# First two graphs of a two-layer graph network: logits as feature columns, broadcasts over all 128 rows, bias from a broadcast tile, products of zeros between stages

## The chip, the core and the metric

The kernel runs on one core of a Trainium2 chip. The metric is device time in microseconds, of one launch over all 64 graphs. A profile is one more execution, taken by the hardware profiler. PE is TensorE (PEld its weight loads), DVE is VectorE, ACT is ScalarE, POOL is GpSimd and SP is the engine whose queue issues nearly all DMAs. Everything is float32, and a matmul of float32 appears in the trace as two records.

## What is computed

There are 64 independent graphs of N = 256 nodes with F = 512 features. Layer 0 is graph attention with H = 8 heads of U = 64 units, layer 1 is dense self-attention with added graph terms; each ends in a residual and a layer norm. Cut to what matters here:

```
feats   = einsum('bnf,hfu->bhnu', X, W)            # layer 0
e_self  = einsum('bhnu,hu->bhn', feats, a_self)
e_neigh = einsum('bhnu,hu->bhn', feats, a_neigh)
dense   = leaky_relu(e_self[..., :, None] + e_neigh[..., None, :], 0.2)
att     = softmax(dense + NEG_BIG * (1 - A), axis=-1)
out     = relu(einsum('bhij,bhju->bhiu', att, feats) + b)
x       = layernorm(x + out)
# layer 1: q, k, v = x @ W_qkv; softmax(q k^T) * LA + LG * adj + LD * exp(-adj), times v;
# x = layernorm(x + result @ W_out + b_out)
```

## The kernel before, in words

**Steady state.** Graphs are handled one after another, in a software pipeline written out by hand: `attention0_beside_projections1(b)` and `attention1_beside_projections0(b)` for b from 2 on mix layer 0 of graph b with layer 1 of graphs b-1 and b-2. There the products of the projections are the seven of Strassen's scheme (`seven`, tiles `pq_p`, `pv_p`, `pf_p`, `po_p`), each `halved` into two matmuls of 64 columns that lie beside each other in the array (line 87).

**The start.** Graphs 0 and 1 go through layer 0 in `start()` and `second_beside_first()` with plain products, because weight sums and the first logits are not there yet. `do(stage, b, step)` records one step, and `in_order()` after it fixes the order of the source on every engine[...]. So the order written in `start()` is the order of PE, DVE, ACT and POOL, and of SP's DMA queue.

The steps of the start that matter below, for graph b = 0 and 1:

- `attention_vectors(g)` (lines 411 to 431) spreads the vectors a_self and a_neigh of four heads over 128 partitions: a matmul of one row of ones, `sel[0:1, H]`, with one row `arow` (line 423, tile `pa_bc`). Ahead of it stand four products of a tile of zeros, `idle` (line 420).
- `logit_weights(g, c, step)` (lines 433 to 449) multiplies the layer's weights by those vectors (`prod`, line 440, on DVE or POOL) and sums over the units (line 446, DVE) into `WA["columns"]`. `vectors_placed` (line 451) copies the sums by ACT into two spare columns per head of the weight tiles `wf`.
- `features(t, g)` (from line 664) makes the features of node tile t and head group g: a matmul of one row that puts the bias in, then four chunks c of 128 input features. `xT_rows` (line 532) turns x first.
- `logits()` (from line 571, matmuls at 575 and 585) makes e_self and e_neigh in matmuls of their own: x against `columns` as rows (40 output rows of 256) and as columns (8 wide).
- `maxima` (lines 594 to 609) takes the row maximum of e_neigh, an exponential, and a small matmul that spreads the maximum (line 599). `factors(g)` (lines 611 to 625) spreads one row per head over 128 partitions: a matmul of 8 rows per head (line 622, tile `pg`). `columns` makes two small exponentials.
- `scaled(h)` (line 688, ACT) moves features from PSUM to SBUF times a factor; `weights(h)` (line 725, DVE, tile `pT`) makes the attention weights of a head; `product(g, t)` (line 748, PE, tile `av`) applies them; `rec0`, `norm0`, `end`, `squares`, `norm` finish layer 0.
- `proj1` with `from_rows` (line 871), `qk` (tile `pq_p`) and `combine_weights1` (lines 278 to 284, DVE sums of weights that `load_weights1` brings in) starts layer 1 of graph 0 beside the second head group of graph 1.

```
def halved(dst, lhsT, rhs, **flags):
    for r in range(2):
        cols = slice(r * (P // 2), (r + 1) * (P // 2))
        matmul(dst[cols], lhsT[:, cols], rhs, **flags)
```

## Time and profile before

| | us |
|---|---|
| median of three runs (2837.8 to 2844.21) | 2844.15 |
| profiled execution, whole | 2843.23 |
| its span, first to last instruction | 2841.4 |
| PE busy in the span | 2823.1 (99%) |
| DVE busy | 2559.0 (90%) |
| ACT busy | 1807.5 (64%) |
| POOL busy | 254.3 (9%) |

From 160 us to 2760 us PE is busy all but 0.7 us; the first layer-1 product (`pq_p`) starts at 64.08 us, and the last 80 us hold one graph's tail. In the table of windows each row gives a stretch, and for each engine the busy time with the number of records, then the granted TensorE clock (1.00 is full speed) and the DMA's share and rate. In the timeline a row has its start, the time to its end, engine, line, operation, tile written and tiles read, and the number of merged records. The chain of work that ended last gives start, share of the time, engine, tile and line of each piece.

### The profile page before, as it was taken

What the parts mean: (1) busy time and instruction counts of PE and PEld (TensorE: products, weight loads), DVE (VectorE), ACT (ScalarE), POOL (GpSimd) and SP (SyncE); (2) the same over time, 40 slices, a digit from 0 to 9 for tenths busy, and PEclk for the clock granted to TensorE, in tenths of its full rate; (3) what the DMA queues carried; (4) which work ended last, traced back from release to release, by engine and by line L of the source; (5) the groups of instructions that cost most, each with busy time, mean ns of one, the idle gap of its engine ahead of it and who ended that gap; (6) DMA issues with size and microseconds to landing.
All of it is one profiled execution on the core that took longest, in us unless ns stands there. A gap on an engine that the chain in (4) does not pass through costs nothing.

```text
span 2841.4 us, 93467 instructions
## 1 busy us (share of the span) xinstructions
PE 2823.1 (99%) x39110; PEld 2241.4 (79%) x39110; DVE 2559.0 (90%) x5125; ACT 1807.5 (64%) x5054; POOL 254.3 (9%) x531
## 2 busy tenths in 40 slices
PE   9999999999999999999999999999999999999998
PEld 6787787887887878887878877888888778778875
DVE  4899999999999999999999999999999999999984
ACT  3656666666666666666666666666666666666664
POOL 1001000000100100010010001001001000100101
PEclk8999999999999999999999999999999999999999
DMA  5445445455454454454454544544544544544532
GB/s 115 102 128 133 126 138 122 132 144 121 130 146 120 127 137 123 131 139 122 136 129 129 140 121 132 144 121 126 140 128 128 139 120 134 136 125 136 125 112 70
DMA packets 773473, 362.82 MB, mean 128 GB/s; under 512 B 689359, under 2 KB 691391, under 8 KB 757054
## 3 DMA queue, kind: packets, MB, share of 16 engines
q1 hardware_dynamic: 770942, 356.33, 47.9%
q8 instruction: 310, 5.08, 0.8%
q14 instruction: 109, 0.89, 0.1%
q10 hardware_dynamic: 2112, 0.52, 0.1%
HBM read 288.37 MB, written 68.13 MB: 125 GB/s over the span
## 4 chain that ended last, share of the span: by engine, by line
PE 98%; DVE 1%; ACT 1%; issue 0%; POOL 0%; POOLq 0%; DVEq 0%; ACTq 0%
PE pq_p L87 27%; PE po_p L87 14%; PE pf_p L87 14%; PE pv_p L87 13%; PE av L748 8%; PE pz L909 8%; PE av L1038 7%; PE pd L948 2%; PE pf L87 1%; PE pr L539 1%; PE po L87 0%; PE pg L622 0%; DVE p L1019 0%; PE pa_bc L423 0%; PE pl L585 0%
## 5 line engine op out<-in xcount | busy, mean ns | idle before, releaser
L87 PE MATMUL pq_p<-hC,wqk_sb 128*64 128x128 f32 x8192 | 470.2, 273 | 1.7 <-ACT qk L337 1.7
L87 PEld LDWEIGHTS pq_p<-hC,wqk_sb 128*64 128x64 f32 x8192 | 448.9, 137 | 3.1 <-ACT qk L337 2.5
L725 DVE SCALAR_TENSOR_TENSOR pT<-gb,ccol,at 128x256 f32<-128x256 f32 x992 | 403.0, 477 | 17.2 <-ACT ccol L639 17.2
L87 PE MATMUL pq_p<-hT,wqk_sb 128*64 128x128 f32 x6144 | 357.9, 273 | 0.7 <-DVE qk L340 0.5
L87 PEld LDWEIGHTS pq_p<-hT,wqk_sb 128*64 128x64 f32 x6144 | 342.3, 137 | 10.5 <-DVE qk L340 0.7
L928 ACT ACTIVATE p<-pz,hide 128x512 f32<-128x512 f32 x638 | 333.2, 629 | 8.9 <-PE pz L909 1.7
L1019 DVE TENSOR_TENSOR p<-p,rb 128x1024 f32<-128x1024 f32 x252 | 298.9, 1206 | 3.4 <-DMA rb<-rs 3.4
L1028 DVE TENSOR_TENSOR p<-p,ct 128x1024 f32<-128x1024 f32 x252 | 299.0, 1207 | 0.2
L769 ACT ACTIVATE x<-av,rec 128x64 f32<-128x64 f32 x1024 | 223.7, 335 | 64.8 <-DVE rec L761 64.8
L748 PE MATMUL av<-v,pT 128*64 128x65 f32 x8192 | 253.6, 222 | 0.6
L87 PE MATMUL pf_p<-wf_sb,xC 128*64 128x264 f32 x1984 | 254.0, 386 | 0.0
L748 PEld LDWEIGHTS av<-v,pT 128*64 128x64 f32 x8192 | 249.8, 138 | 2.6 <-issue 2.0
L87 PE MATMUL pv_p<-wv_sb,hC 128*64 128x256 f32 x2048 | 244.4, 379 | 2.6 <-ACT v L337 2.5
L337 ACT COPY qk<-pq_p 128x512 f32<-128x512 f32 x256 | 148.8, 581 | 152.2 <-PE pq_p L87 148.5
L1038 PE MATMUL av<-p,v 128*64 128x256 f32 x2016 | 241.2, 380 | 2.1 <-DVE p L1028 2.1
L688 ACT ACTIVATE v<-v 128x64 f32<-128x64 f32 x992 | 243.0, 336 | 0.0
L909 PE MATMUL pz<-qk 64*128 64x256 f32 x2048 | 239.4, 384 | 0.0
L337 ACT COPY v<-pv_p 128x256 f32<-128x256 f32 x256 | 95.7, 374 | 221.0 <-PE pv_p L87 221.0
L87 PE MATMUL po_p<-wo_sb,oC 128*64 128x256 f32 x1984 | 235.2, 379 | 0.0
L391 POOL TENSOR_SCALAR rstd_l<-rstd_l 128x2 f32<-128x2 f32 (+1 forms) x130 | 95.6, 736 | 1536.1 <-ACT junk L380 1535.9
L909 PEld LDWEIGHTS pz<-qk 64*128 64x128 f32 x2048 | 192.9, 187 | 45.6 <-issue 25.0
L940 DVE SCALAR_TENSOR_TENSOR both<-p 128x512 f32<-128x512 f32 x256 | 172.2, 674 | 45.1 <-ACT p L928 44.8
(169 smaller groups left out, 4480.7 us busy)
## 6 DMA issues: line engine op xcount, KB each, us to landing
rb<-rs SPq DMA_DIRECT2D x63, 1024.0 KB
gb<-gs SPq DMA_DIRECT2D x62, 1028.0 KB
hs<-x SPq DMA_DIRECT2D x64, 512.0 KB
xb<-in_x_dram SPq DMA_DIRECT2D x252, 128.0 KB
x<-in_x_dram SPq DMA_DIRECT2D x63, 512.0 KB
y<-hs SPq DMA_DIRECT2D x63, 512.0 KB
out_dram<-y SPq DMA_DIRECT2D x63, 512.0 KB
hb<-hs SPq DMA_DIRECT2D x248, 128.0 KB
```

Of the source, the lines that this page charges most:

```text
L87: matmul(dst[cols], lhsT[:, cols], rhs, **flags)
L337: nc.scalar.copy(out[COPIES[p]], dst)
L688: nc.scalar.activation(v[:, :U], src, AF.Copy, scale=v[:, U : U + 1])
L725: nc.vector.scalar_tensor_tensor(pT[h][:, j, :], GB[b][h], CCOL[b][:, j, h : h + 1], AT[b][:, j, :], op0=ALU.max, op1=ALU.mult,)
L748: matmul(av[r * half : (r + 1) * half, k, :], pT[h][:, j, i : i + half], V0[b][:, j, h, :UA], start=(j == 0), stop=(j == T - 1),)
L769: nc.scalar.activation(X1[b][:, t, h * U : (h + 1) * U], av[:, k, :U], AF.Copy, scale=REC0[g][:, t, k : k + 1],)
L909: matmul(pz[r][:, j, :], QK[b][rows, g, 1, j * P : (j + 1) * P], QK[b][rows, g, 0, :], start=True, stop=True,)
L928: nc.scalar.activation(to, of, AF.Exp, bias=hide[:, j, b : b + 1], scale=U**-0.5,)
L940: nc.vector.scalar_tensor_tensor(both[g], p[:, :, 0, :], TINY, p[:, :, 1, :], op0=ALU.add, op1=ALU.add)
L1019: nc.vector.tensor_mul(p, p, REC[b][:, k : k + 2, g // 2, :] .unsqueeze(2) .to_broadcast([P, 2, T, N]),)
L1028: nc.vector.tensor_add(p, p, CT[b].unsqueeze(1).to_broadcast([P, 2, T, N]))
L1038: matmul(av[0][r * U : (r + 1) * U, g % 2, :], V1[b][:, j, 2 * g + r, :], PROBS[b][g][:, r, j, :], start=(j == 0), stop=(j == T - 1),)
```

## The change

It touches `start()`, the steps that `start()` records for graphs 0 and 1, and one step of the second stage. Nothing of the steady state is changed but where one set of weight sums is made.

- `sel`, `arow` and `grow` get 128 rows, with zeros where there were none, and the matmuls of `pa_bc`, `pg` and the small maximum's `sel` copy read all of them (the maximum's matmul itself keeps 8 rows). The memsets for it are on DVE and POOL; the rows of `arow` are loaded after x.
- The sums of `logit_weights` go directly into the spare columns of `wf`, and `features` takes all 66 columns per head: features and logits come out of one product of 264 columns. `logits()` loses its matmuls and becomes four small copies; four transposes (tile `pr`) turn the logits into rows.
- The bias matmul of one row inside `features` goes. `bias_rows` spreads the bias once (one matmul of 512 columns), and `copied` adds it while moving features out of PSUM (DVE); `scaled` then works on SBUF.
- `keep_busy(dst, n)` issues n products of the zero tile: 8 at the start in place of 4, 8 and 2 in graph 0's `maxima`, 6 in graph 1's.
- The order in `start()` is rewritten. Among others the second half of graph 1's factors, weights and scalings now stand behind the first `pq_p` products.
- `right_factors(wo_sb, ...)` (four DVE sums) moves from `second_beside_first()` into the stage of b = 2, and the tile `wo12` takes another buffer.

```diff
-    arow = wo_sb[0:1, 4:].rearrange("p k c f -> p k (c f)")
+    arow = wo_sb[:, 4:].rearrange("p k c f -> p k (c f)")
+    nc.vector.memset(arow[:, 0], 0.0)
+    nc.gpsimd.memset(arow[:, 1], 0.0)
+    nc.gpsimd.memset(arow[:, 2], 0.0)
...
-    sel = work.tile([H, H + 1, P], FT, tag="rb", name="sel", bufs=1)
+    sel = work.tile([P, H + 1, P], FT, tag="rb", name="sel", bufs=1)
...
-        wo12 = work.tile([P, C2, F2], FT, tag="pT", name="wo12", bufs=4)
+        wo12 = work.tile([P, C2, F2], FT, tag="p", name="wo12", bufs=5)
...
+    def bias_rows():
+        pb = WA["bias"].rearrange("p k h u -> p (k h) u")
+        matmul(
+            pb.rearrange("p h u -> p (h u)"), sel[:, H, :], arow[:, 2], start=True, stop=True
+        )
+        nc.scalar.copy(b0_bc[:, :, :U], pb)
+        in_order()
+
+    def keep_busy(dst, n):
+        for _ in range(n):
+            matmul(dst, idle, idle, start=True, stop=True)
...
             nc.vector.tensor_reduce(
-                WA["columns"][:, c, :, g * HG : (g + 1) * HG], WA.pop((g, c)), AX.X, ALU.add
-            )
+                wf[c // C2][g][:, c % C2, :, U:].rearrange("p h s -> p s h"),
+                WA.pop((g, c)),
+                AX.X,
+                ALU.add,
+            )
...
+        def logits(g):
...
+                nc.vector.tensor_copy(
+                    ROW["near"][:, t, :, g * HG : (g + 1) * HG],
+                    PF[t, g][:, :, U:].rearrange("p h s -> p s h"),
+                )
+        def maxima(part=None):
+            if part == 1:
+                matmul(ROW["max"], sel[:H, H, :], ROW["diag"], start=True, stop=True)
+                if b == 0:
+                    keep_busy(WA[1][:, 0, :2], 2)
+                return
...
+                    transpose(ps[:, s, t * P : (t + 1) * P], ROW["near"][:, t, s, :])
+            if b == 0:
+                keep_busy(WA[1][:, 0, :2], 8)
...
+                matmul(
+                    pg[:, k, :], sel[:, h + k, :], ROW["rows"][:, :N], start=True, stop=True
+                )
...
-                PF[t, g] = ps_tile([P, HG, U], f"pf_{b}_{t}_{g}")
-                halved(
-                    PF[t, g],
-                    sel[0:1, H, :],
-                    arow[:, 2, g * HG * U : (g + 1) * HG * U],
-                    start=True,
-                    stop=False,
-                )
+                PF[t, g] = ps_tile([P, HG, UX], f"pf_{b}_{t}_{g}")
...
+        def copied(t, g):
+            nc.vector.tensor_add(
+                halves(t, g)[:, :, :U],
+                PF.pop((t, g))[:, :, :U],
+                b0_bc[:, g * HG : (g + 1) * HG, :U],
+            )
```

The new order in `start()`, cut to its second half (`do` left out): `factors` of two heads, `scaled`, `weights` for graph 0's heads 0 to 3; `factors` for heads 4 to 7; `product` 0; `copied` for the second group; `xT` of graph 1; `rec0`, `scaled`, `masks`, `norm0`, `far`; `features` of graph 1's first group; `weights` 4 to 7; `product` 1; `logits` 0; `combine_weights1(0)`; `rec0`, `norm0` and `features` of the second group; `end`, `squares`, `copied`, `logits` 1, `norm`, `maxima`, six products of zeros, `norm`, `from_rows` 0, `copied`, the maximum, `columns`, `factors` 0 to 3, `shared`, `aT`, `pq_p` p1, `from_rows` 1, `far`, p2, `hC`, `combine_weights1(4)`, p6, `combine_weights1(1)`, `scaled` and `weights` 0 to 3, p5, p7, `combine_weights1(2)`, `factors` 4 to 7, `scaled` and `weights` 4 to 7, `shared`, p4, p3.

More of the change, by code (lines that the diff above doesn't have):

```diff
@@ L147, in load_rows @@
         nc.sync.dma_start(X[b], x[b].rearrange("(t p) f -> p t f", p=P))
+    rowmask = consts.tile([P, NB // B, N // B, B], FT, name="rowmask")
+    idle = rowmask[:, 0, : P // B].rearrange("p i b -> p (i b)")
+    nc.vector.memset(idle, 0.0)
     wo_sb = consts.tile([P, 7, C2, F2], FT, name="wo_sb")
-    arow = wo_sb[0:1, 4:].rearrange("p k c f -> p k (c f)")
-    for k, a in enumerate((a_self, a_neigh, b0)):
-        nc.sync.dma_start(arow[:, k, :], a.rearrange("h u -> (h u)").unsqueeze(0))
+    arow = wo_sb[:, 4:].rearrange("p k c f -> p k (c f)")
+    nc.vector.memset(arow[:, 0], 0.0)
+    nc.gpsimd.memset(arow[:, 1], 0.0)
+    nc.gpsimd.memset(arow[:, 2], 0.0)
     X[0] = io.tile([P, T, F], FT, tag="hb", name="x_0", bufs=1)
@@ L156 @@
         nc.sync.dma_start(X[0][:, t, :], x[0, t * P : (t + 1) * P, :])
+    for k, a in enumerate((a_self, a_neigh, b0)):
+        nc.sync.dma_start(arow[0:1, k, :], a.rearrange("h u -> (h u)").unsqueeze(0))
     wf_sb = consts.tile([P, 7, C2, HG, UX], FT, name="wf_sb")
@@ L171 @@
     load_wf(nc.sync, 1)
-    sel = work.tile([H, H + 1, P], FT, tag="rb", name="sel", bufs=1)
+    sel = work.tile([P, H + 1, P], FT, tag="rb", name="sel", bufs=1)
     nc.vector.memset(sel[:, H, :], 1.0)
-    rowmask = consts.tile([P, NB // B, N // B, B], FT, name="rowmask")
-    idle = rowmask[:, 0, : P // B].rearrange("p i b -> p (i b)")
-    nc.vector.memset(idle, 0.0)
     load_adj(0)
@@ L180 @@
     nc.vector.memset(b0_bc, 0.0)
-    nc.sync.dma_start(
-        b0_bc[:, :, :U], b0.rearrange("h u -> (h u)").partition_broadcast(P)
-    )
     wqk_sb = consts.tile([P, 7, C2, F], FT, name="wqk_sb")
@@ L191 @@
     nc.vector.tensor_copy(
-        sel[:, :H, :], ident[:H, :H].unsqueeze(2).to_broadcast([H, H, P])
+        sel[:, :H, :], ident[:, :H].unsqueeze(2).to_broadcast([P, H, P])
     )
@@ L212, in masks @@
             maskf = work.tile([NB, N], FT, tag="far", name="maskf", bufs=1)
+            MASK["rows"] = maskf
             nc.scalar.copy(maskf, mask_sb)
+        elif step == 1:
+            maskf = MASK.pop("rows")
             nc.vector.transpose(maskz, maskf)
@@ L414, in attention_vectors @@
         if g == 0:
-            WA["psum"] = psum.tile([P, 2, 2, HG, U], FT, tag="sc", name="pa_bc", bufs=2)
             WA["sbuf"] = io.tile([P, 2, 2, HG, U], FT, tag="x1", name="a_bc", bufs=1)
-            WA["columns"] = work.tile([P, C, 2, B], FT, tag="hC", name="wa", bufs=1)
-            nc.vector.memset(WA["columns"], 0.0)
-            for _ in range(4):
-                matmul(WA["psum"][:, 0, 0, :2], idle, idle, start=True, stop=True)
+        pa = WA[g] = psum.tile([P, 2, 2, HG, U], FT, tag="sc", name=f"pa_bc_{g}", bufs=2)
+        WA["bias"] = pa[:, 1]
+        pa = WA[g] = pa[:, 0]
+        if g == 0:
+            keep_busy(pa[:, 0, :2], 8)
         for k in range(2):
@@ L423, in attention_vectors @@
             matmul(
-                WA["psum"][:, g, k].rearrange("p h u -> p (h u)"),
-                sel[0:1, H, :],
+                pa[:, k].rearrange("p h u -> p (h u)"),
+                sel[:, H, :],
                 arow[:, k, cols],
@@ L429, in attention_vectors @@
             )
-        nc.scalar.copy(WA["sbuf"][:, g], WA["psum"][:, g])
+        nc.scalar.copy(WA["sbuf"][:, g], pa)
         in_order()
+    def bias_rows():
[8 more added lines that the diff above has]
+            matmul(dst, idle, idle, start=True, stop=True)
     def logit_weights(g, c, step):
@@ L438, in logit_weights @@
             )
-            engine, src = (nc.gpsimd, "sbuf") if c % 2 or g and c else (nc.vector, "psum")
+            engine, src = (
+                (nc.gpsimd, WA["sbuf"][:, g]) if c % 2 else (nc.vector, WA[g])
+            )
             engine.tensor_mul(
@@ L442, in logit_weights @@
                 wf[c // C2][g][:, c % C2, :, :U].unsqueeze(1).to_broadcast([P, 2, HG, U]),
-                WA[src][:, g],
+                src,
             )
@@ L446, in logit_weights @@
             nc.vector.tensor_reduce(
-                WA["columns"][:, c, :, g * HG : (g + 1) * HG], WA.pop((g, c)), AX.X, ALU.add
-            )
-        in_order()
-    def vectors_placed():
-        for k in range(2):
-            for g in range(2):
-                nc.scalar.copy(
-                    wf[k][g][:, :, :, U:].rearrange("p c h s -> p c s h"),
-                    WA["columns"][:, k * C2 : (k + 1) * C2, :, g * HG : (g + 1) * HG],
-                )
+                wf[c // C2][g][:, c % C2, :, U:].rearrange("p h s -> p s h"),
+                WA.pop((g, c)),
+                AX.X,
+                ALU.add,
+            )
         in_order()
@@ L569, in proj0 @@
         ROW = {}
-        def logits():
-            pl = ps_tile([P, 2, N], f"pl_{b}")
-            for c in range(C):
-                matmul(
-                    pl[: B + H, 0],
-                    WA["columns"][:, c].rearrange("p s k -> p (s k)")[:, : B + H],
-                    xT[:, c],
-                    start=(c == 0),
-                    stop=(c == C - 1),
-                )
-            near = pl[:, 1, : T * H].rearrange("p (t h) -> p t h", h=H)
-            for t in range(T):
-                for c in range(C):
-                    matmul(
-                        near[:, t],
-                        xT[:, c, t * P : (t + 1) * P],
-                        WA["columns"][:, c, 1, :H],
-                        start=(c == 0),
-                        stop=(c == C - 1),
-                    )
-            ROW.update(logits=pl, near=near, max=pl[:, 1, T * H : (T + 1) * H])
+        def logits(g):
+            if g == 0:
+                ROW["near"] = small.tile([P, T, 2, H], FT, tag="lg", name=f"lg_{b}", bufs=1)
+            for t in range(T):
+                nc.vector.tensor_copy(
+                    ROW["near"][:, t, :, g * HG : (g + 1) * HG],
+                    PF[t, g][:, :, U:].rearrange("p h s -> p s h"),
+                )
@@ L594, in maxima, with cleared @@
+        def cleared():
+            ROW["rows"] = small.tile([P, N + 1], FT, tag="grow", name=f"grow_{b}", bufs=1)
+            nc.gpsimd.memset(ROW["rows"], 0.0)
         def maxima(part=None):
             if part == 1:
-                nd = ROW["nd"] = small.tile([P, T, H], FT, tag="nd", name=f"nd_{b}", bufs=2)
-                nc.vector.tensor_copy(nd, ROW["near"])
-                matmul(ROW["max"], sel[:, H, :], ROW["diag"], start=True, stop=True)
+                matmul(ROW["max"], sel[:H, H, :], ROW["diag"], start=True, stop=True)
+                if b == 0:
+                    keep_busy(WA[1][:, 0, :2], 2)
@@ L600, in maxima @@
                 return
-            pl = ROW["logits"]
-            grow = small.tile([H, N + 1], FT, tag="grow", name=f"grow_{b}", bufs=1)
+            pr = psum.tile([P, 2, 2, N], FT, tag="sc", name=f"pr_{b}", bufs=2)
+            ps = pr[:H, 0]
+            for s in range(2):
+                for t in range(T):
+                    transpose(ps[:, s, t * P : (t + 1) * P], ROW["near"][:, t, s, :])
+            if b == 0:
+                keep_busy(WA[1][:, 0, :2], 8)
+            grow = ROW["rows"]
@@ L603, in maxima @@
             nb = small.tile([H, 1], FT, tag="nb", name=f"nb_{b}", bufs=2)
-            nc.vector.tensor_reduce(grow[:, N : N + 1], pl[B : B + H, 0], AX.X, ALU.max)
-            nc.vector.tensor_scalar_mul(nb, grow[:, N : N + 1], -0.8)
-            nc.scalar.activation(grow[:, :N], pl[:H, 0], AF.Exp, bias=nb, scale=-0.8)
+            nc.vector.tensor_reduce(grow[:H, N : N + 1], ps[:, 1, :], AX.X, ALU.max)
+            nc.vector.tensor_scalar_mul(nb, grow[:H, N : N + 1], -0.8)
+            nc.scalar.activation(grow[:H, :N], ps[:, 0, :], AF.Exp, bias=nb, scale=-0.8)
@@ L607, in maxima @@
             diag = small.tile([H, H], FT, tag="diag", name=f"diag_{b}", bufs=1)
-            nc.vector.tensor_scalar_mul(diag, ident[:H, :H], grow[:, N : N + 1])
-            ROW.update(rows=grow, diag=diag)
-        def factors(part=None):
-            grow = ROW["rows"]
-            if part != 1:
-                nc.vector.tensor_scalar(
-                    grow[:, :N], grow[:, :N], 1.0, TINY, op0=ALU.min, op1=ALU.max
-                )
-                GB[b] = []
-            for g in range(2) if part is None else (part,):
-                pg = psum.tile([P, HG, N], FT, tag="sc", name=f"pg_{b}_{g}", bufs=2)
-                for k in range(HG):
-                    matmul(
-                        pg[:, k, :], sel[:, g * HG + k, :], grow[:, :N], start=True, stop=True
-                    )
-                    GB[b].append(pg[:, k, :])
+            nc.vector.tensor_scalar_mul(diag, ident[:H, :H], grow[:H, N : N + 1])
@@ new lines, in maxima, with clamped, busy, factors @@
+            ROW.update(diag=diag, max=pr[:, 1, 0, :H])
+        def clamped():
+            nc.vector.tensor_scalar(
+                ROW["rows"][:H, :N], ROW["rows"][:H, :N], 1.0, TINY, op0=ALU.min, op1=ALU.max
+            )
+            GB[b] = []
+        def busy(n):
+            ROW["pg"] = psum.tile([P, HG, N], FT, tag="sc", name=f"pg_{b}_0", bufs=2)
+            keep_busy(ROW["pg"][:, 0, :P], n)
+        def factors(h, n):
+            if "pg" in ROW:
+                pg = ROW.pop("pg")
+            elif n == 2:
+                pg = ps_tile([P, n, N], f"pg_{b}_{h}")
+            else:
+                pg = psum.tile([P, n, N], FT, tag="sc", name=f"pg_{b}_{h}", bufs=2)
+            for k in range(n):
+                matmul(
+                    pg[:, k, :], sel[:, h + k, :], ROW["rows"][:, :N], start=True, stop=True
+                )
+                GB[b].append(pg[:, k, :])
@@ L627, in columns @@
         def columns():
-            if b > 1:
-                nd = small.tile([P, T, H], FT, tag="nd", name=f"nd_{b}", bufs=2)
-            else:
-                nd = ROW["nd"]
+            nd = small.tile([P, T, H], FT, tag="nd", name=f"nd_{b}", bufs=2)
             nc.vector.tensor_sub(
                 nd,
-                V0[b][:, :, :, U + 1] if b > 1 else nd,
+                V0[b][:, :, :, U + 1] if b > 1 else ROW["near"][:, :, 1, :],
                 (gb[:, :, N] if b > 1 else ROW["max"])
@@ L666, in features @@
             if c is None or c == 0:
-                PF[t, g] = ps_tile([P, HG, U], f"pf_{b}_{t}_{g}")
-                halved(
-                    PF[t, g],
-                    sel[0:1, H, :],
-                    arow[:, 2, g * HG * U : (g + 1) * HG * U],
-                    start=True,
-                    stop=False,
-                )
+                PF[t, g] = ps_tile([P, HG, UX], f"pf_{b}_{t}_{g}")
             for c in range(C) if c is None else (c,):
@@ L678, in features @@
                     xT[:, c, t * P : (t + 1) * P],
-                    wf[c // C2][g][:, c % C2, :, :U],
-                    start=False,
+                    wf[c // C2][g][:, c % C2],
+                    start=(c == 0),
                     stop=(c == C - 1),
                 )
+        def copied(t, g):
[4 more added lines that the diff above has]
+            )
         def scaled(h):
@@ L686, in scaled @@
                 v = V0[b][:, t, h]
-                src = v[:, :U] if b > 1 else PF[t, h // HG][:, h % HG]
-                nc.scalar.activation(v[:, :U], src, AF.Copy, scale=v[:, U : U + 1])
+                nc.scalar.activation(v[:, :U], v[:, :U], AF.Copy, scale=v[:, U : U + 1])
         return dict(
+            copied=copied,
+            cleared=cleared,
             logits=logits,
             maxima=maxima,
+            busy=busy,
+            clamped=clamped,
             factors=factors,
@@ L1212, in start @@
         attention_vectors(1)
+        do("proj0", 0, "xT_rows")
         for step in (
@@ L1222, in start @@
             (1, 1, 0),
+            (1, 0, 0),
+            (1, 3, 0),
+            (1, 0, 1),
             (1, 2, 0),
-            (1, 0, 0),
-            (1, 0, 1),
             (1, 1, 1),
-            (1, 3, 0),
             (1, 2, 1),
-            (1, 3, 1),
         ):
             logit_weights(*step)
-        do("proj0", 0, "xT_rows")
-        for c in range(C):
-            for t in range(T):
-                do("proj0", 0, "features", t, 0, c)
-        masks(0)
-        masks(1)
-        do("proj0", 0, "logits")
-        for c in range(2):
-            do("proj0", 0, "features", 0, 1, c)
-        do("proj0", 0, "maxima")
+            if step[2] == 1:
+                for t in range(T):
+                    do("proj0", 0, "features", t, *step[:2])
+            if step == (1, 2, 0):
+                bias_rows()
+                masks(0)
+            if step == (1, 2, 1):
+                do("proj0", 0, "logits", 0)
+        logit_weights(1, 3, 1)
+        for t in range(T):
+            do("proj0", 0, "features", t, 1, 3)
         do("proj0", 0, "aT")
@@ L1245, in start @@
         combine_weights1 = load_weights1()
+        do("proj0", 0, "logits", 1)
+        do("proj0", 0, "cleared")
+        do("proj0", 0, "maxima")
+        do("proj0", 0, "copied", 0, 0)
+        do("proj0", 0, "copied", 1, 0)
         do("proj0", 0, "maxima", 1)
-        for c in range(2, C):
-            do("proj0", 0, "features", 0, 1, c)
+        do("proj0", 0, "clamped")
         do("proj0", 0, "columns")
-        do("proj0", 0, "factors", 0)
-        do("proj0", 0, "factors", 1)
-        do("proj0", 0, "features", 1, 1)
         for h in range(HG):
+            if h % 2 == 0:
+                do("proj0", 0, "factors", h, 2)
             do("proj0", 0, "scaled", h)
             do("attend0", 0, "weights", h)
-        do("proj0", 0, "far", 1)
+        do("proj0", 0, "factors", HG, HG)
         for t in range(T):
             do("attend0", 0, "product", 0, t)
+        do("proj0", 0, "copied", 0, 1)
+        do("proj0", 0, "copied", 1, 1)
         do("turned", 1, "xT")
@@ L1263, in start @@
             do("proj0", 0, "scaled", h)
+        masks(1)
+        masks(2)
         do("attend0", 0, "norm0", 0, 0)
         do("attend0", 0, "norm0", 0, 1)
-        do("attend0", 0, "weights", HG)
-        do("attend0", 0, "weights", HG + 1)
-        do("proj0", 1, "logits")
-        vectors_placed()
-        do("proj0", 1, "maxima")
-        do("attend0", 0, "weights", HG + 2)
-        do("attend0", 0, "weights", HG + 3)
+        do("proj0", 0, "far", 1)
         for t in range(T):
             do("proj0", 1, "features", t, 0)
-        do("proj0", 1, "maxima", 1)
+        for h in range(HG, H):
+            do("attend0", 0, "weights", h)
         for t in range(T):
             do("attend0", 0, "product", 1, t)
-        do("proj0", 1, "columns")
-        do("proj0", 0, "shared", 0)
-        do("proj0", 1, "aT")
-        do("proj0", 1, "far", 0)
-        do("proj0", 1, "factors", 0)
+        do("proj0", 1, "cleared")
+        do("proj0", 1, "logits", 0)
+        combine_weights1(0)
         do("attend0", 0, "rec0", 1)
@@ L1285, in start @@
             do("attend0", 0, "norm0", 1, t)
+            do("proj0", 1, "features", t, 1)
+        for t in range(T):
             do("attend0", 0, "end", tiles[t])
-        do("attend0", 0, "squares", tiles[0])
-        do("attend0", 0, "squares", tiles[1])
         for t in range(T):
-            do("proj0", 1, "features", t, 1)
-        do("proj0", 1, "factors", 1)
-        for h in range(HG):
-            do("proj0", 1, "scaled", h)
+            do("attend0", 0, "squares", tiles[t])
+        do("proj0", 1, "copied", 0, 0)
+        do("proj0", 1, "copied", 1, 0)
+        do("proj0", 1, "logits", 1)
         do("attend0", 0, "norm", tiles[0])
+        do("proj0", 1, "maxima")
+        do("proj0", 1, "busy", 6)
         do("attend0", 0, "norm", tiles[1])
         do("proj1", 0, "from_rows", 0)
+        do("proj0", 1, "copied", 0, 1)
+        do("proj0", 1, "copied", 1, 1)
+        do("proj0", 1, "maxima", 1)
+        do("proj0", 1, "clamped")
+        do("proj0", 1, "columns")
+        do("proj0", 1, "factors", 0, HG)
+        do("proj0", 0, "shared", 0)
+        do("proj0", 1, "aT")
+        do("proj1", 0, "qk", "p1")
         do("proj1", 0, "from_rows", 1)
@@ L1299, in start @@
         load_rows(1)
-        for h in range(HG):
-            do("attend0", 1, "weights", h)
-        do("proj1", 0, "qk", "p1")
-        combine_weights1(0)
-        combine_weights1(4)
+        do("proj0", 1, "far", 0)
         do("proj1", 0, "qk", "p2")
         do("proj1", 0, "hC")
+        combine_weights1(4)
         do("proj1", 0, "qk_add", 11)
@@ L1309, in start @@
         combine_weights1(1)
+        for h in range(HG):
+            do("proj0", 1, "scaled", h)
+            do("attend0", 1, "weights", h)
+        do("proj1", 0, "qk", "p5")
+        do("proj1", 0, "qk", "p7")
+        combine_weights1(2)
+        do("proj0", 1, "factors", HG, HG)
+        do("proj1", 0, "qk_add", 22)
+        for h in range(HG, H):
+            do("proj0", 1, "scaled", h)
+        for h in range(HG, H):
+            do("attend0", 1, "weights", h)
         do("proj0", 0, "shared", 1)
@@ L1312, in start @@
         load_adj(2)
-        do("proj1", 0, "qk", "p5")
-        do("proj1", 0, "qk", "p7")
-        for h in range(HG, H):
-            do("proj0", 1, "scaled", h)
-            do("attend0", 1, "weights", h)
-        combine_weights1(2)
-        do("proj1", 0, "qk_add", 22)
         do("proj1", 0, "qk", "p4")
@@ L1338, in second_beside_first @@
         do("turned", 2, "xC")
-        for t in range(T):
-            do("attend0", b, "norm0", 0, t)
+        do("attend0", b, "norm0", 0, 0)
         do("proj1", 0, "values", "p1")
+        do("attend0", b, "norm0", 0, 1)
         for t in range(T):
@@ L1372, in second_beside_first @@
         do("proj0", 2, "add", 11)
-        right_factors(wo_sb, WO["12"], (0, 1))
         do("proj0", 2, "add", 12)
@@ L1378, in second_beside_first @@
         do("proj0", 2, "rows")
-        right_factors(wo_sb, WO.pop("12"), (2, 3))
         do("proj0", 2, "broadcast", 0)
@@ L1449, in attention0_beside_projections1 @@
         do("attend1", b - 3, "residual")
+        if b == 2:
+            right_factors(wo_sb, WO["12"], (0, 1))
         do("proj1", b - 1, "values", "p6")
@@ L1455, in attention0_beside_projections1 @@
             do("attend1", b - 3, "sum_up", t)
+        if b == 2:
+            right_factors(wo_sb, WO.pop("12"), (2, 3))
         if b + 2 < NB:
```

## The prediction

> **What bounds the kernel now.** I read the page first, for the engines over the span:

> ```profile
> PE   9999999999999999999999999999999999999998
> PEclk8999999999999999999999999999999999999999
> ```

> PE is full from the first slice to the last, and nothing else is; but one slice has a clock below nine tenths, the first 71 us. So time is PE time, and the change lies where PE is full and slow. The chain of waits agrees: PE holds 98% of it. The windows of 10 us show where (columns: busy of PE, PEld, DVE, ACT, POOL with records, granted clock, DMA share, GB/s):

> ```profile
> 20.00:30.00 10.00, 9.95 (x50) 6.62 (x49) 1.84 (x7) 4.29 (x15) 0.00 (x0) 0.71 0.25 45
> 30.00:40.00 10.00, 10.00 (x95) 6.44 (x94) 4.41 (x10) 1.54 (x7) 0.00 (x0) 0.61 1.15 225
> 40.00:50.00 10.00, 10.00 (x58) 5.61 (x58) 4.13 (x13) 2.63 (x13) 0.00 (x0) 0.73 0.75 132
> ```

> DVE and ACT are less than half busy there: PE is the limit at a clock of 0.6 to 0.7. Windows of 2 us date it: the clock is 0.50 from about 24.4 to 37.9 us and from 44.8 to 51.6 us. The PE timeline tells what ran, and that the first stretch was slow too, although its clock is given as 1.00:

> ```profile
> 12.97 5.39 PE L87 MATMUL pf<-wf_sb,xT 128*64 128x256 f32 x28
> 22.87 1.08 PE L87 MATMUL pf<-wf,xT 128*64 128x256 f32 x8
> ...
> 26.29 7.19 PE L622 MATMUL pg<-grow,sel 8*128 8x256 f32 x16
> 33.41 1.12 PE L87 MATMUL pf<-wo_sb,sel 1*64 1x256 f32 x4
> ```

> Eight `pf` records take 1.08 us at 22.87, but between 13.4 and 17.3 their weight loads come two every 0.43 us, 0.215 per record, just as at 34.9 to 37.1, where the clock is given as 0.50. The 8-row `pg` records take 0.45 us here and 1.99/8 = 0.25 at 54 us. So three stretches run at half speed: 1.2 to 17.5 (0.65 idle in it), 24.4 to 37.9, 44.8 to 51.6. PE time in them is 15.7 + 13.5 + 6.8 = 36 us, half of it, 18.0 us, is lost. In the chain, the pieces that the change removes or turns:

> ```profile
> 18.63 1.85 PE pl L575 x8
> 20.48 1.90 PE pl L585 x16
> ...
> 39.92 1.72 PE pl L575 x8
> 41.64 1.88 PE pl L585 x16
> ...
> 64.08 3.74 PE pq_p L87 x64
> ```

> **Which work keeps the clock down.** The changes lie 6.8 us apart or twice that (17.5, 24.4, 37.9, 44.8, 51.6). The rises come at the end of a stretch of nothing but full 128-row `pf` products (14.1 to 17.5, 34.5 to 37.9, 48.1 to 51.6); stretches with 1-row or 8-row products, or products 8 columns wide, end in a fall or in no rise, with PE busy 10.00 of 10. [...]rows or columns of the array in use count in some way.[...]

> **Part by part, PE** (prices at full clock). Removed: eight 1-row bias products in `features`, each 0.57 in the chain (22.29 to 22.87 starts, 43.45 to 44.03): 4.6. `logits` twice: (1.85 + 1.90) + (1.72 + 1.88) = 7.4. Together 12.0. Added: 264 columns for 256, 0.06 x 8 = 0.5 (`pf_p` 0.89 against `pv_p` 0.86 for eight records, two such per call). `bias_rows`, 512 columns, twice a `pg` product of 0.49: 0.9. Eight transposes, 0.11 each by the 43-row `pr` ones (0.44 for four): 0.9. Twenty more products of zeros, 0.52 each at half clock (2.08 for four): 0.26, so 5.2. Together 7.5. The 128-row `pg` and `pa_bc` cost what they cost now[...]. Against: less than 0, no reason for it; more, up to a few tenths.

> **DVE, ACT, POOL, queues.** DVE gains eight `copied` (0.41 each, the `v` add from PSUM), eight small copies (0.17), one product that was POOL's (0.68): 5.4 us; it loses `nd` copies and the `wa` memset (0.6). POOL's memsets: the 128x128 one takes 0.20, so under 1 us each; ident, behind two of them, is wanted only at 5 us. ACT loses `vectors_placed` (0.9). On SP x goes ahead of `arow`; issue of x is 1.73, and a row landed about 2 us after issue, so `pa_bc` starts near 5.4 in place of 3.2. The eight zero products (8 x 0.52 from 1.2) cover exactly that. SP behind it (mask, wf, adj, xb) loses the 256 KB bias broadcast; adj 1 and 3 MB of weights follow graph 0's `aT`, at 16.6 in place of 23.1, so the weights for `combine_weights1(0)`, which by DMA rates were complete near 38, come near 31: just in time for DVE at 32.

> **The new start, walked** with those durations[...]. `pa_bc` to 8.4 (its second group no longer waits for ACT's copy), x transposed 9.4, in SBUF 10.1. Sixteen `pf` steps of 0.445 and the bias: 7.1 + 0.9 gives 18.2. DVE alongside: twelve products and sums of about 0.62 from 8.0, with copies and `aT` to 16.6, so PE is last by little. Small copies, transposes 19.0; maximum, exponential, clamp (0.42 + 0.15 + 0.46 + 0.27 with hand-offs): 20.6, but PE stands in eight zero products to 21.1, the maximum 21.5, two more zero products 22.0: they cost 1.4 here. Two factors 23.0, four heads of `pT` on DVE 3.2: 26.2 (before: 33.4). `av` 28.0; DVE two `copied`, `xT` 28.1; features of graph 1's first group 31.9, beside `pT` 28.7 to 31.9; `av` 33.9; second group 37.5. `norm0`, `end`, `squares` on ACT and POOL end beside it (norm at 38.3). Transposes 38.4, six zero products 40.0, first half of `from_rows` 40.3, maximum 40.7, four factors 41.7. **`pq_p` starts at 41.7, before at 64.1: 22.4 earlier.** A second account: 64.1 less 18.0 of clock, less 12.0, plus 7.5, less 2.3 (second factors and half of `from_rows` now later), plus 3.0 for the first 6 us that stay half: 42.3. They agree.

> Given back behind it: from there to the end of graph 1's `av` (before 64.1 to 81.7, 17.6 us, DVE and PE taking turns) DVE now has, after its maximum, `shared` 1.0, `aT` 0.7, `hC` 1.5 (which waits until 44.8 for the second half of hT), weight sums 1.2 x 3, three adds of 0.68, sixteen `pT` 6.4, `shared` 1.5, `wv` sums 2.5: last at 62.2, `av` at 62.9. That is 21.2 us, 3.6 more. Net 18.8. Hand-offs that the walk leaves out, some 16 of 0.05 to 0.1 us, take 1.0 to 1.3. `right_factors(wo_sb)`: two of its sums lie on the chain at 97 to 98 (1.2); in the stage of b = 2 it adds 2.7 to DVE, which is 8.3 busy of 10 at 120 to 130 with PE at 10.00. Hidden there; uncovered it would cost up to 2.7. Taken as nothing. From 160 us on PE is never idle, so what the start gains arrives at the end.

> Sum: 2843.2 - 17.5 = 2825.7 for a profiled execution; the median of runs stands 0.9 above it: **2826.5 us**.

> **What is not shown.** Whether zeros in all 128 rows count as activity: between nothing (the clock behaves as now) and all. The nearest rows are the `idle` products at 1.17, 2.08 us long[...]. The 1-row products show that used rows matter, not that data does; I take them as counting.

> **Rivals.**
> 1. Zeros don't count: the change doesn't do what it says, though its removed work stays. The clock rises only after real `pf` products: near 17.5, so `pf` ends 4.6 later; it falls again during `pg` (4 us of it at half: +4.0) and returns in graph 1's features (+1.7). Gain 17.5 - 10.3 = 7.2: 2837. For it: rises came with real data only. Chance 14%.
> 2. DVE becomes the bound: the walk already has DVE at 21.2 us from p1 to `av`; if `combine_weights1(0)` waits for its weights (in `start()` it stands ahead of `rec0`, and behind that `norm0`, `end`, the whole norm) by 3 us, and the moved `wo` sums cost 2.7: 2832. Against: 31 before 32. Chance 13%.
> 3. Slower: the clock stays half all through the start, because the products are now interleaved with DVE's sums (each pair of `pf` waits for one) and with padded ones[...]. PE's 35.8 us up to `pq_p` become 71.6, start at 73: 9 later than now, and 3.6 behind it: 2857. It decides at 18.8 us more of PE work done at half clock than the 3.0 that I allow. Against: sixteen real `pf` steps at half clock take 14 us and wait for nothing. Chance 4%.

> **Numbers.** Main case 69%, 2819 to 2832: [...]DVE's 3.6 may not appear, the zero products (2.4 on the path) may hide. Within 0.3% (8.5 us; about what a measurement of this kernel can tell from no change) lies most of rival 1 and some of a worse rival 2. Faster 0.86, same 0.10, slower 0.04. Range 2817 to 2837.

> **What would show it.** Clock: windows of 10 us from 10 to 60 at 0.95 to 1.00, `pg` records 0.25. Start: first `pq_p` near 42, `pT` of graph 0 from 23. Turn: `av` of graph 1 ending near 63. Wrong if 0.50 returns beside `pg` or zero products (rival 1), if the first weight sum waits for a DMA (rival 2), or if PE idles in the stage of b = 2.

## The result, and the profile after

The changed kernel takes 2827.35 us (median of four runs, 2826.8 to 2827.65), before 2844.18 (four runs, 2837.8 to 2845.14). The ratio is 0.9945, with a 95% interval of 0.9928 to 0.9963: 16.8 us or 0.55% faster. The forecast was 2826.5, the range 2817 to 2837. In one kernel below (the kernel before with 128 rows alone) one run of four took 4168.03 us at a mean granted clock of 0.654; it is left out of that kernel's median, and its cause is open. The profiled execution took 2827.07 us, its span 2825.3, against 2843.23 and 2841.4.

The page, for PE and its clock over the 40 slices. The first slice of the clock is a nine now; PE is as full as it was:

```profile
PE   9999999999999999999999999999999999999998
PEclk9999999999999999999999999999999999999999
```

The changed kernel's windows of 10 us (busy of PE, PEld, DVE, ACT, POOL with records, granted clock, DMA share, GB/s), which answer to 0.71, 0.61 and 0.73 of before:

```profile
20.00:30.00 10.00, 9.81 (x115) 7.85 (x116) 8.13 (x23) 6.50 (x29) 0.32 (x1) 1.00 1.02 191
30.00:40.00 10.00, 9.02 (x130) 6.84 (x124) 6.15 (x21) 5.77 (x17) 2.34 (x8) 1.00 1.04 186
40.00:50.00 10.00, 8.41 (x112) 7.35 (x114) 6.36 (x12) 2.82 (x7) 0.00 (x0) 1.00 0.66 157
```

The clock is full, and in exchange PE idles, up to 1.6 us in ten, and DVE is busier: what was hidden under slow matmuls now shows. From the changed kernel's timeline, the pieces that answer to those of before:

```profile
1.04 3.78 PE L448 MATMUL pa_bc<-rowmask 128*128 128x128 f32 x16 [1.04 <-DVE rowmask L152]
...
12.83 1.06 PE L87 MATMUL pf<-wf,xT 128*64 128x264 f32 x8
...
21.11 3.62 PE L638 MATMUL pg<-grow,sel 128*128 128x256 f32 x16
...
42.09 1.97 PE L87 MATMUL pq_p<-hT,wqk_sb 128*64 128x128 f32 x32
```

Sixteen `pg` records take 3.62 us where they took 7.19. `pq_p` starts at 42.09 (before 64.08; the prediction said 41.7). The trace's clock records show one rise, at 5.0 us, and no fall before 2790 us. In the 3.4 us ahead of that rise PE ran nothing but the zero products that start at 1.04, for 3.2 us, and waited: here products of zeros raised the clock.

The lead over before, read from the starts of the same tiles in both traces, is 22.0 us at `pq_p`, 19.0 at the first `pv_p` (81.70 against 62.73), 18.0 at the first `pf_p`, 17.9 at the first `po_p` (122.5 in the changed kernel), about 17.5 through the steady state and 16.1 at the end of these two executions.

### The profile page after: what moved, and what is told of

Read it like the earlier page. It is cut to its first block, busy times and chain, and to the rows that moved or that the text cites. A ratio compares the mean times of both kernels' runs of the same rounds, so it can differ in the third digit from the quotient of the medians.

```text
span 2825.3 us, 93442 instructions
## 1 busy us (share of the span) xinstructions
PE 2802.8 (99%) x39080; PEld 2238.0 (79%) x39080; DVE 2564.2 (91%) x5140; ACT 1811.0 (64%) x5051; POOL 257.3 (9%) x534
## 2 busy tenths in 40 slices
PE   9999999999999999999999999999999999999998
## 3 DMA queue, kind: packets, MB, share of 16 engines
q1 hardware_dynamic: 769902, 356.07, 48.1%
## 4 chain that ended last, share of the span: by engine, by line
PE 96%; DVE 1%; DMA 1%; SPq 1%; ACT 1%; issue 0%; POOL 0%; DVEq 0%; POOLq 0%
PE pq_p L87 27%; PE po_p L87 14%; PE pf_p L87 14%; PE pv_p L87 13%; PE av L764 8%; PE pz L925 8%; PE av L1054 7%; PE pd L964 2%; PE pr L551 1%; PE po L87 0%; SPq L265 0%; DMA rb<-rs 0%; DMA wo_sb<-in_L_gnn_W_out_dram 0%; SPq L244 0%; SPq L123 0%
## 5 line engine op out<-in xcount | busy, mean ns | idle before, releaser
L87 PE MATMUL pq_p<-hC,wqk_sb 128*64 128x128 f32 x8192 | 470.7, 273 | 3.1 <-DVE wqk_sb L283 1.6
L87 PEld LDWEIGHTS pq_p<-hC,wqk_sb 128*64 128x64 f32 x8192 | 449.1, 137 | 5.0 <-issue 3.1
L87 PE MATMUL pq_p<-hT,wqk_sb 128*64 128x128 f32 x6144 | 358.2, 273 | 0.3 <-DVE qk L343 0.3
L87 PEld LDWEIGHTS pq_p<-hT,wqk_sb 128*64 128x64 f32 x6144 | 342.5, 137 | 10.3 <-issue 0.8
L87 PE MATMUL pf_p<-wf_sb,xC 128*64 128x264 f32 x1984 | 254.5, 386 | 0.0
L700 ACT ACTIVATE v<-v 128x64 f32<-128x64 f32 x1024 | 251.3, 337 | 2.6 <-DVE v L691 2.6
L87 PE MATMUL pv_p<-wv_sb,hC 128*64 128x256 f32 x2048 | 245.3, 380 | 3.7 <-ACT v L340 3.7
L87 PE MATMUL po_p<-wo_sb,oC 128*64 128x256 f32 x1984 | 235.2, 379 | 0.0
```

What stands on the lines that cost most here:

```text
L700: nc.scalar.activation(v[:, :U], v[:, :U], AF.Copy, scale=v[:, U : U + 1])
```

## Experiments

Two theories stood after the result. **A**: the clock follows the rows of the array in use (the length of the contraction), whatever the data, so the 128 rows and the zero products made the gain. **B**: the gain is the removed work and the new order; zeros only stand in the way. All times below are medians of a kernel and of the kernel before that ran beside it; where a start of a tile is given, it is from one profile.

### Without products of zeros

```diff
     def keep_busy(dst, n):
-        for _ in range(n):
-            matmul(dst, idle, idle, start=True, stop=True)
+        return
```

> The changed kernel without any product of zeros (24 matmuls left out; they feed nothing). Theory A (the clock follows how much of the array is in use, whatever the data): the first rise slips from 5 us to the first full window of real products, 9 to 14 us, [...]later PE idles 1 to 2 us where the zeros stood, with no fall: 2 to 5 us slower than the changed kernel. Rival B (the gain is removed work and order; zeros only stand in the way): 1 to 2.5 us faster, since two groups of zeros lie on the path.

Measured: 2827.54 us (before 2844.24; ratio 0.9945, 0.993 to 0.996), the same as the changed kernel. The first rise comes at 11.6 us in place of 5.0, as A said; `pf` starts at 10.82 in place of 8.97. But `pg` starts only 1.2 later and `pq_p` 0.25 later (42.34):

```profile
10.82 4.15 PE L87 MATMUL pf<-wf_sb,xT 128*64 128x264 f32 x32
...
22.33 3.69 PE L637 MATMUL pg<-grow,sel 128*128 128x256 f32 x16
```

No fall comes in its first 60 us (1.00 in every window of 10 us). So the zeros raised the clock early, and what they gained there they cost later, where `pg` and `pq_p` stand behind them (0.6 and 1.0 us won back). Neither theory's time was right (2 to 5 us slower, 1 to 2.5 faster): the two effects cancel.

### Few rows again, with and without zeros

```diff
-                sel[:, H, :],
-                arow[:, k, cols],
+                sel[0:1, H, :],
+                arow[0:1, k, cols],
...
-                    pg[:, k, :], sel[:, h + k, :], ROW["rows"][:, :N], start=True, stop=True
+                    pg[:, k, :], sel[:H, h + k, :], ROW["rows"][:H, :N], start=True, stop=True
```

(`bias_rows` likewise.) With zeros:

> The changed kernel, where the matmuls of pa_bc, bias_rows and factors read 1 and 8 rows again; zero products stay. Theory A: rise at 5 us as now, but the clock returns to 0.50 behind the 8-row factors of graph 0 (21 to 25 us) for at least one stretch of 6.8 us: 3 to 8 us slower than the changed kernel. Rival B: same time within 1 us, factor records at 0.25 us.

Measured: 2832.13 us (four runs, 2827.95 to 2832.47; before 2844.24; ratio 0.9956, 0.9939 to 0.9972), 4.8 slower than the changed kernel's 2827.35, as A said. Its windows, the same stretches as above, and its `pg` record from the timeline:

```profile
20.00:30.00 10.00, 9.94 (x76) 7.86 (x74) 6.95 (x20) 4.12 (x17) 0.32 (x1) 0.83 1.02 181
30.00:40.00 10.00, 10.00 (x154) 7.63 (x152) 5.66 (x16) 4.89 (x22) 0.00 (x0) 0.83 0.97 182
40.00:50.00 10.00, 9.99 (x82) 7.74 (x78) 5.33 (x18) 4.90 (x13) 2.32 (x8) 0.85 0.54 137
```

```profile
23.86 4.57 PE L638 MATMUL pg<-grow,sel 8*128 8x256 f32 x16
```

The clock is 0.50 from 26.6 to 33.4 us, from the middle of the 8-row products on, and from 47.0 to 50.5, behind graph 1's. The first rise slips to 12.9: the zeros are the same, but the 1-row `pa_bc` follows them. Both undone at once:

> Both undone at once: 1-row and 8-row matmuls, no zero products; the removed work and the order stay. Theory A: two or three stretches at half clock as in the kernel before, 8 to 14 us slower than the changed kernel, so about 2836 to 2841. Rival B: within 2 us of the changed kernel.

Measured: 2835.41 us (eight runs, 2831.87 to 2839.22; ratio 0.997, 0.9959 to 0.998), 8.1 slower than the changed kernel, at A's edge. First rise at 14.9, 0.50 from 25.1 to 35.3 and from 49.0 to 52.4. So the removed work and the order without the rows keep 8.8 us: part of B stands.

### The kernel before, with 128 rows alone

```diff
-    arow = wo_sb[0:1, 4:].rearrange("p k c f -> p k (c f)")
+    arow = wo_sb[:, 4:].rearrange("p k c f -> p k (c f)")
+    nc.vector.memset(arow[:, 0], 0.0)
+    nc.gpsimd.memset(arow[:, 1], 0.0)
+    nc.gpsimd.memset(arow[:, 2], 0.0)
...
-            grow = small.tile([H, N + 1], FT, tag="grow", name=f"grow_{b}", bufs=1)
+            grow = small.tile([P, N + 1], FT, tag="grow", name=f"grow_{b}", bufs=1)
+            nc.gpsimd.memset(grow, 0.0)
```

(`sel` gets 128 rows too, and the matmuls of `pa_bc`, the bias and `pg` read them.)

> The kernel before with only the 128 rows (zero-filled) in its vectors', bias and factors' matmuls; its own logits matmuls and order stay. Theory A: the first rise comes at 7 to 11 us in place of 17.4, and the fall at 24.4 goes or shortens: 5 to 13 us faster than before. Rival B: within 1 us of before.

Measured: 2828.68 us (three runs, 2828.01 to 2829.31; ratio 0.9948, 0.9931 to 0.9964), 15.6 faster than before: nearly the whole gain, more than A's 5 to 13, and B, which gave the rows nothing, is out. The first rise comes at 4.6 us, sooner than A's 7 to 11, and no fall follows in the start, with the old order and the old logits still there:

```profile
20.00:30.00 10.00, 10.00 (x114) 7.53 (x112) 6.11 (x14) 5.81 (x28) 0.31 (x1) 1.00 0.79 160
30.00:40.00 10.00, 9.95 (x128) 7.90 (x128) 4.49 (x14) 2.63 (x13) 0.00 (x0) 1.00 1.03 202
40.00:50.00 10.00, 9.76 (x98) 7.28 (x98) 8.43 (x18) 6.78 (x22) 2.32 (x8) 1.00 0.58 128
```

Its PE timeline, with the products 8 columns wide still in it and the same `pg` at full speed:

```profile
12.82 2.31 PE L578 MATMUL pl<-xT,wa 128*40 128x256 f32 x8
15.06 1.95 PE L588 MATMUL pl<-wa,xT 128*128 128x8 f32 x16
...
20.05 3.72 PE L626 MATMUL pg<-grow,sel 128*128 128x256 f32 x16
...
47.86 3.71 PE L87 MATMUL pq_p<-hT,wqk_sb 128*64 128x128 f32 x64 [0.24 <-ACT hT L875]
```

`pq_p` starts at 47.86: with the rows alone the lead is 16.2 of the 22.0 us, and the rest of the change adds 5.8. At `pv_p` (65.49) the lead is still 16.2, while the changed kernel's has shrunk to 19.0: half of what the rest gained is gone there.

### Zeros of 8 rows

```diff
-            matmul(dst, idle, idle, start=True, stop=True)
+            matmul(dst, idle[:H], idle[:H], start=True, stop=True)
```

> The changed kernel, its zero products cut from 128 to 8 rows (they feed nothing). Theory A (rows in use count, data doesn't): [...]first rise at 9 to 14 us in place of 5; the later ones lie among 128-row work, no fall or one window. Rival C (any product counts, and 1-row bias products were slow for another reason): rise at 5 us as now. Time in both within 2 us of the changed kernel, so the clock's first rise in the trace decides.

Measured: 2830.28 us (three runs, 2830.09 to 2832.3; before 2843.03; ratio 0.9957, 0.9942 to 0.9973), 2.9 slower than the changed kernel, where both theories said within 2. From its PE timeline, the same products as in the changed kernel but for the rows, in the same 3.78 us, and `pg`:

```profile
1.04 3.78 PE L448 MATMUL pa_bc<-rowmask 8*128 8x128 f32 x16 [1.04 <-DVE rowmask L152]
...
23.11 5.41 PE L638 MATMUL pg<-grow,sel 128*128 128x256 f32 x16
```

The first rise comes at 10.5 us in place of 5.0, as A said. But this rise, which was to decide, does not: the stretches of the clock lasted whole multiples of 3.41 us (last section), and counted back so from 10.5 us a rise could have come at 3.7, with 2.62 us of the zeros ahead of it, or at 7.1, with 1.2 us of them and 1.2 of `pa_bc` in the 3.41 us ahead. The rises behind 128-row zeros followed more, 3.2 us in the changed kernel and 2.9 in the last kernel below. That the rows made the difference at the start was not shown. The later zeros decide. The 0.50 returns from 24.1 to 27.6, at `pg`: the 3.41 us ahead of it held 2.2 us of 8-row zeros and 1.03 of 128-row `pg`. In the changed kernel the same zeros with 128 rows stood ahead of `pg` and no fall came: `pg` took 3.62 us there and 5.41 here, 1.8 more for one stretch of 3.41 us at 0.50. So the rows counted here, and zeros with 128 rows counted too: A. The kernel without any zeros did not have this fall; the last section tells how near to it it came.

### Weight sums into DVE's gap

The turn, in the changed kernel's timeline: DVE waits 3.31 us for hT, then does four `hC` sums and the weight sum L283, and PE waits for that.

```profile
45.30 0.43 DVE L304 TENSOR_TENSOR hC<-hT 128x256 f32<-128x256 f32 x1 [3.31 <-ACT hT L887]
...
46.77 1.22 DVE L283 TENSOR_TENSOR wqk_sb<-wqk_sb 128x1024 f32<-128x1024 f32 x1
...
48.13 5.46 PE L87 MATMUL pq_p<-hC,wqk_sb 128*64 128x128 f32 x96 [1.59 <-DVE wqk_sb L283]
```

```diff
         do("proj0", 1, "aT")
+        combine_weights1(4)
+        combine_weights1(1)
         do("proj1", 0, "qk", "p1")
...
         do("proj1", 0, "hC")
-        combine_weights1(4)
...
         do("proj1", 0, "qk", "p6")
-        combine_weights1(1)
```

> The changed kernel with two weight sums (combine parts 4 and 1, 1.2 us each on DVE) moved from behind hC to ahead of the first layer-1 product, into the 3.3 us in which DVE waits for hT. Theory (DVE sets the pace from 42 to 63 us, which is the 3 us given back): 1.2 to 2.4 us faster than the changed kernel. Rival (PE's and ACT's own order sets it): within 0.6 us.

Measured: 2828.02 us (2826.01 to 2828.55; before 2843.03; ratio 0.9947, 0.993 to 0.9964): no gain in the median. Its timeline shows the stall gone:

```profile
42.44 1.18 DVE L283 TENSOR_TENSOR wqk_sb<-wqk_sb 128x1024 f32<-128x1024 f32 x1
...
45.82 0.42 DVE L304 TENSOR_TENSOR hC<-hT 128x256 f32<-128x256 f32 x1 [1.06 <-ACT hT L887]
...
47.06 3.17 PE L87 MATMUL pq_p<-hC,wqk_sb 128*64 128x128 f32 x54
```

From the start of `pq_p` to that of `pf_p` it takes 24.95 us (42.61 to 67.56) in place of 26.4 (42.09 to 68.47): 1.4 saved, the theory's size, in one profile of each. But `pq_p` itself started 0.5 later. What is left is under the scatter of the runs, so a gain in time is not shown. Then ACT's steps:

```diff
-        for t in range(T):
-            do("attend0", b, "norm0", 1, t)
         do("proj1", 0, "values", "p2")
         do("proj1", 0, "v_add", 11)
+        do("proj1", 0, "values", "p6")
+        for t in range(T):
+            do("attend0", b, "norm0", 1, t)
         do("attend0", b, "end")
         right_factors(wf_sb, wf12, (0, 1, 2))
-        do("proj1", 0, "values", "p6")
```

> As the one before, and graph 1's second half of norm0 (8 small ACT steps of 0.22) behind the copies of the values' products p2 and p6, for which PE waits at 65 to 67.5 us. Theory (ACT order costs PE about 1 us there): a further 0.5 to 1.2 us. Rival: end then comes later on DVE and its weight sums for graph 2's features make PE wait instead: no gain, or 1 us slower.

Measured: 2826.67 us (ratio 0.9942, 0.9927 to 0.9957), not to be told from the changed kernel. The PE timeline shows the rival at work: PE now waits 0.83 us for graph 2's weight sums instead,

```profile
67.08 1.06 PE L87 MATMUL pf_p<-wf_sb,xT 128*64 128x264 f32 x8
...
69.83 1.11 PE L87 MATMUL pf_p<-wf_sb,xC 128*64 128x264 f32 x8 [0.83 <-DVE wf_sb L234]
```

and graph 1's next product, `ph`, 8.05 us behind the first `pf_p` in the kernel without this step, is 9.1 behind it here.

### The output weights' sums back in their old place

```diff
-        if b == 2:
-            right_factors(wo_sb, WO["12"], (0, 1))
...
-        if b == 2:
-            right_factors(wo_sb, WO.pop("12"), (2, 3))
...
         do("proj0", 2, "add", 11)
+        right_factors(wo_sb, WO["12"], (0, 1))
...
         do("proj0", 2, "rows")
+        right_factors(wo_sb, WO.pop("12"), (2, 3))
```

> The changed kernel with the four wo sums back in the second stage. By the prediction the move is worth nothing: within 0.7 us. Rival: the two sums that stood on the chain at 97 us cost 1.2 us there: 1.0 to 1.5 us slower; or the stage of b = 2 suffers from them: 0.5 to 2.7 us faster.

Measured: 2827.1 us (before 2843.03; ratio 0.9946, 0.9931 to 0.9961), within 0.3 of the changed kernel. The move is worth nothing in time, as predicted.

### Zeros at the start alone, weight sums early

```diff
-            if b == 0:
-                keep_busy(WA[1][:, 0, :2], 8)
...
-        do("proj0", 1, "busy", 6)
```

This has the 8 zero products at the start and none later (the two behind the maximum go too), with the weight sums early. Beside it ran the changed kernel once more.

> The changed kernel itself, as the partner for the one beside it. Every theory: 2826.5 to 2828.

> The changed kernel with the two weight sums early, and with the 8 zero products at the start but none later (16 matmuls that feed nothing are left out). Theory (later zeros only stand ahead of the small maximum on PE, 1 to 2.3 us, and the clock holds without them since nothing has few rows): 1.5 to 3.5 us faster than the changed kernel run beside it. Rival (without them [...]the clock falls once): equal, or up to 2 us slower, with a 0.50 between 20 and 45 us.

Measured: the changed kernel 2827.14 (2826.63 to 2828.62); this one 2825.47 (five runs: 2825.11, 2825.12, 2825.47, 2827.06, 2830.47), with 2843.8 for before (ratio 0.9945, 0.9932 to 0.9957). The median is 1.7 us lower, but one run of five is 3.3 us above the changed kernel's median, and the intervals overlap: a gain is not shown. Two things differ here from the changed kernel, so the 1.7 can't be parted either. The profile tells why both theories have a share:

```profile
20.00:30.00 10.00, 9.88 (x103) 7.77 (x104) 7.68 (x20) 6.57 (x29) 0.32 (x1) 0.83 1.08 194
```

`pg` starts at 20.21, 0.9 earlier, and then runs partly at half speed: without the zeros the clock fell for one stretch of 3.4 us (20.9 to 24.4). Run by run the mean clock was 0.998 or 0.999 at 2825 us, 0.997 at 2827 and 0.996 in the one of 2830. So the later zeros look like insurance: in these runs they cost about what they save.

## Why the prediction was right

**The time** is off by 0.9 us. **The walk** stands: `pq_p` 42.09 against 41.7, graph 1's `av` ends at 62.9 as predicted, graph 0's `pT` starts at 22.3 against 23.0, the norm at 38.3 as predicted. The first `pf` came 1.1 us sooner than the walk had it (8.97 against 10.1), as the clock rose at 5.0, where the walk, by an estimate of its author's, had the first 6 us from 1.2 on at half speed, and `combine_weights1(0)` took that back: DVE waited 1.54 us for its weights, until 32.88 (the walk: 32). The DMA that rival 2 named was there, at half its price. That these two cancel is luck, and so may be a part of the 0.9: the mean clock was 0.999 in this execution and 0.998 in two of the other three runs.

**Clock and work.** The second account had 15.0 us of clock and 6.8 of work and of steps moved behind. Measured at `pq_p`: 16.2 for the rows alone, 5.8 for the rest. Both sizes hold, to 1.2 us. The times do not add: rows alone 15.6, the rest alone 8.8, both 16.8. Two things in the traces account for it. Without the 1-row products between them, the rest alone has 3.41 us of nothing but real `pf` products ahead of a rise at 14.9, and its slow stretches are shorter too (half speed up to 14.9 us, then 0.50 for 10.2 and 3.4; before: up to 17.4, then for 13.7 and 6.8). And with both, DVE sets the pace behind `pq_p`: 20.6 us from there to `pv_p`, 17.6 with rows alone. This is the 3.6 us that the prediction gave back; it measured 3.0.

**Zeros counted** (with 128 rows): right, by the rise at 5.0 us behind nothing but zeros, and by the fall at 24.1 where they had 8 rows. Rival 1 (14%) is out. **Their price**, 2.4 us on the path, was right in kind too: without the later ones `pg` starts 0.9 us sooner.

**What the rows do not tell.** In the trace of before, the falls at 24.2 and 44.7 us are not the rows' alone. The 3.41 us ahead of them held only 0.76 and 0.58 us of products with 1 or 8 rows, while 1.59 us of them from 54.9 to 58.3 were followed by no fall. What both held is 1.5 and 1.9 us of the products 8 columns wide, as the prediction had read it:

```profile
20.41 1.95 PE L585 MATMUL pl<-wa,xT 128*128 128x8 f32 x16
22.29 0.65 PE L87 MATMUL pf<-wo_sb,sel 1*64 1x256 f32 x4
...
41.57 1.95 PE L585 MATMUL pl<-wa,xT 128*128 128x8 f32 x16
43.45 0.65 PE L87 MATMUL pf<-wo_sb,sel 1*64 1x256 f32 x4
```

Either kind alone tells the same. With 128 rows in the kernel before, 1.9 us of these products beside 1.5 us of wider ones were followed by no fall (14.8 to 18.2 and 28.5 to 31.9 us). With few rows and without these products, falls followed 2.8 and 2.1 us of 8-row ones (23.1 to 26.6 and 43.6 to 47.0 us, few rows with zeros). What sorts the changes of the first 72 us, in the traces of before and of the changed kernel, is how long products of 128 rows and more than 8 columns ran in the 3.41 us ahead (last section), and the change takes away most of both other kinds. That is a count on two traces; no run was made to test it.

**What was wrong.** The 1.0 to 1.3 us for hand-offs: none was missing up to 62.9. Instead 1.0 went between `pv_p` and `pf_p`, where a copy on ACT stands behind `norm0` (5.74 us from one to the other, before 4.79), and 0.4 to 1.8 by the end. That last part is not settled; one place in it is the wait for `rb`, 4.8 us in all against 3.4.

Rival 3 did not come: the clock rose at 5.0 us and stayed full through the start.

## What to carry to other kernels

A full PE was not a fast PE here (busy 10.00 of 10 at a clock of 0.61, before, from 30 to 40 us): read the granted clock beside the busy time in windows of a few us, and where it is 0.50 look at how many rows the matmuls there read and how few columns they have. Padding the contraction to 128 rows with zeros cost nothing per matmul here (eight `pg` records 1.99 us with 8 rows and with 128) and was worth 15.6 us here, alone, in 17 changed lines. With the clock full, the next gains (removed matmuls, a better order) went partly to the engine that was hidden under the slow matmuls, here DVE (of 5.8 us at `pq_p` 2.8 were left at `pv_p`), so walk the next 20 us before counting them.
